# Two graph layers on one Trainium2 core: own issue tables for the second and the last-but-one graph, a last head in two pieces, an input check in steps, and sums scaled on GpSimd

## The chip, the core and the metric

The kernel runs on one core of one Trainium2 chip. The metric is the time of one execution in microseconds (us), as the device measures it; the time before is the median of three runs. Beside it there is one execution taken by the hardware profiler, and every duration below comes from that one.

The engines are named as in the profile: PE is the matrix engine (PEld its loading of weights), DVE the vector engine, ACT the scalar engine, POOL the GpSimd engine, and SP the engine from whose queue the DMAs of this kernel are issued. Each engine takes its instructions strictly in the order in which they were issued to it, and an instruction that waits holds up everything behind it on the same engine.

## The reference

There are 16 graphs of 1024 nodes with 256 features, and an adjacency matrix of integers for each. Two layers follow each other, each with a residual and a normalisation over the features.

```python
# layer 0: gated sum over all nodes; the gate depends on the kind of the edge
e = leaky(einsum('bid,bjd->bij', h * a[:, 0], h))          # four of these, a0 to a3
alpha = sigmoid(where(adj == 1, e0, where(adj == 2, e1, ... , neg_inf)))
x = layernorm(x + einsum('bij,bjd->bid', alpha, h) + bias)
# layer 1: graph attention with 4 heads of 64 features
Wh = (x @ W).reshape(B, N, 4, 64)
s = leaky_relu(e_src[:, :, None, :] + e_dst[:, None, :, :], 0.2)
alpha = softmax(where(A > 0, s, -1e9), axis=2)
x = layernorm(x + elu(einsum('bijh,bjhf->bihf', alpha, Wh)))
```

The adjacency of the data holds zeros and ones only and is symmetric. The kernel has a fast path for that, notes during the run whether the inputs allow it, and reads one flag at the end; if the flag is set, a general path computes everything again. With these data the flag is clear.

## The kernel before

**Stages and tables.** `stages` (L194) holds, for one graph, about fifty generators, one for each step of the work: `score`, `leak`, `leaky`, `sigmoid`, `below`, `lower`, `upper`, `self_loop` and `agg` for layer 0; `project`, `wh`, `product`, `high`, `low`, `pos`, `acc`, `acc_low`, `acc_sum`, `total`, `weigh`, `divide`, `elu` and `join` for layer 1; `moments`, `gathered`, `spread`, `shift` and `norm` for the normalisations. A table gives for each step of each generator a place on a common axis. Graph `b` is moved by `b` times `PERIOD` (112.0), all steps of all graphs are sorted, and `issue` (L1290) runs them in that order. So the tables, written out by hand as numbers, decide the order of the instructions on each engine, and nothing is reordered later. Several graphs are in work at once: while one is in layer 1, the next one is in layer 0. Before the change there are three tables: `FIRST` for graph 0, `LAST` for graph 15, and `TIMES` for graphs 1 to 14.

**The softmax as two sums.** In layer 1 the exponential of the leaky sum is one of two products, depending on whether the sum is positive. `pos` (L659, DVE) writes a 128 x 512 tile of zeros and ones for a head, half of the nodes and a block of 128 neighbours. `acc` (L671, PE) multiplies it with the factors `gm`, which hold a high and a low part of each number. `acc_low` (ACT) and `acc_sum` (L694, DVE) add the two parts into the tile `u`. The two PSUM tiles of `acc` are given back by these two steps, and the next head's first matmul needs them. `pos` has six buffers.

**The steps that the change touches in the middle graphs.** For each half of the nodes and each of its two pairs of blocks, `weigh` subtracts (L752 or L777) and then multiplies the second sum with `rho`; `divide` adds the sums (L787), takes the reciprocal of the denominator (L790, L792) and multiplies the sum with it; `elu` (L809, ACT) and `join` (L801, L803, DVE) follow. Both multiplications are the function `times`:

```python
if late:    # the last two graphs
    ... nc.scalar.activation(val[:, q, h, :], val[:, q, h, :], AF.Copy, scale=by[:, q, h : h + 1])
else:
    by = by.unsqueeze(3).to_broadcast(list(val.shape))
    nc.vector.tensor_tensor(val, val, by, ALU.mult)          # L769
```

So a graph has eight of these instructions on DVE, four on 128 x 520 numbers and four on 128 x 512, and graphs 0 to 13 have 112.

**GpSimd.** Apart from a few instructions that make constants, POOL runs only `spread` (L468 and L469), which turns four variances into four reciprocal square roots: twice in each layer of each graph.

**The last graph.** It computes layer 1 in another way: `pos_last` (L862) writes weights in full precision, `acc_last` (L872) multiplies them with the head's factors into a 65 x 512 sum, `kept_last` (L884, ACT) copies it, `turned_last` (L890, PE) turns it in four blocks, `inverse_last` (L904, L905), `scale_last` (L923, ACT), `elu_last` (L940), `join_last` (L947, L949) follow, and then the normalisation: four nodes' blocks at a time, with `spread` on POOL.

**The check.** After all graphs the kernel compares three kinds of numbers with their limits (L1470 to L1488: the sums of the adjacency and of its square, the span of the scores, the largest reciprocal), turns the result across the partitions on PE, and writes `flag`. Every engine then loads the flag (L1490) and branches over the general path.

Of the kernel before, what the change touches and what calls it, by code (L numbers as in the profile page):

```python
# [21 lines left out]
EPS = 1e-5  # L22
# [25 lines left out]
def make_constants(nc, k, const, work):  # L48
    D = k.D
    k.ident = const.tile([P, P], F32, name="ident")  # L50
    make_identity(nc, k.ident)
    k.ident16 = const.tile([P, P], BF16, name="ident16")
    make_identity(nc, k.ident16)
    k.mhalf = const.tile([P, 1], F32, name="mhalf")
    nc.gpsimd.memset(k.mhalf, -0.5)
    k.ones_r = const.tile([P, P], F32R, name="ones_r")
    ones = work.tile([P, P], F32, tag="ones", name="ones")
    nc.gpsimd.memset(ones, 1.0)
    nc.scalar.copy(k.ones_r, ones)
    k.ones = k.ones_r.bitcast(F32)  # L60
    k.w_aug = const.tile([P, k.DC, k.WD], F32, name="w_aug")
    k.bias_bc = const.tile([P, D], F32, name="bias_bc")
# [131 lines left out]
def stages(nc, k, pl, b, xg, adjg, outg, sums, span, zinv):  # L194
# [297 lines left out]

    def yt():
# [265 lines left out]
    def times(val, by):  # L759
# [7 lines left out]
        else:  # L767
            by = by.unsqueeze(3).to_broadcast(list(val.shape))
            nc.vector.tensor_tensor(val, val, by, ALU.mult)  # L769
# [87 lines left out]

    def pos_last():
        for half, h in LAST_HEADS:
            for jb in range(NB):  # L860
                p_ = t["pos", half, h, jb] = pl.pos.tile([P, HALF], F32, tag="pos", name="pos")
                nc.vector.scalar_tensor_tensor(  # L862
                    p_, t["sbc", half, h], t["es"][:, 1, jb, h : h + 1],
                    t["mT"][:, jb, half * HALF : (half + 1) * HALF], ALU.max, ALU.mult,
                )
                yield

    def acc_last():
        for half, h in LAST_HEADS:
            acc = t["acc", half, h] = pl.ps_u.tile([P, 2, HALF], F32, tag="u", name="acc")  # L870
            for jb in range(NB):
                nc.tensor.matmul(  # L872
                    acc[0 : F + 1, 0, :],
                    lhsT=factor_of(h)[:, jb],
                    rhs=t["pos", half, h, jb],
# [5 lines left out]
    def kept_last():  # L881
        for half, h in LAST_HEADS:
            kept = t["kept", half, h] = pl.allm.tile([P, HALF], F32, tag="allm", name="kept")
            nc.scalar.copy(kept[0 : F + 1, :], t["acc", half, h][0 : F + 1, 0, :])  # L884
            yield

    def turned_last():
        for half, h in LAST_HEADS:
            for q in range(NQ):
# [10 lines left out]
    def inverse_last():  # L900
        t["rz"] = pl.small.tile([P, H, NB], F32, tag="rzs", name="rzs")
        for half, h in LAST_HEADS:
            rz = t["rz"][:, h, half * NQ : (half + 1) * NQ]
            nc.vector.tensor_scalar(rz, sums_of(half, h)[:, :, F], Z_MIN, None, ALU.max)  # L904
# [47 lines left out]
    def leave():  # L952
        for half in range(NH):
# [5 lines left out]
            if half == NH - 1:  # L959
                z = zinv.rearrange("p b h -> p h b") if last else zinv  # L960
                nc.vector.tensor_tensor(z, z, t["rz"], ALU.max)
            yield

# [16 lines left out]
        spread1=spread("1"), shift1=shift("1"), norm1=norm("1"), leave=leave(),  # L980
# [110 lines left out]
FIRST = {  # L1091
    "aload": [-146.50, -146.40, -145.60, -145.40, -145.20, -144.50],
    "cast": [-146.00, -145.00, -144.10, -143.30, -142.40, -141.30, -140.80, -140.10],
    "turn": [-145.50, -144.80, -144.00, -143.00, -141.90, -140.90, -140.30, -139.30],
    "mask": [-145.10, -144.30, -142.70, -142.60, -141.20, -140.50, -139.70, -139.00],
    "setup": [-145.90, -142.90, -140.70],
    "xt": [-147.40, -147.20, -146.90, -146.80],
    "xtc": [-147.10, -146.70, -146.30, -146.10],
    "xta": [-146.60, -145.70, -144.70, -143.40, -141.50, -140.90, -139.60, -138.50],
    "score": [  # L1100
        -146.20, -144.90, -144.40, -143.70, -143.10, -142.30, -142.00, -141.80, -140.40,
        -139.10, -138.80, -137.70,
    ],
    "leak": [
        -145.80, -144.60, -143.90, -143.50, -142.80, -142.20, -141.40, -140.60, -140.00,
        -138.40, -138.10, -137.30,
    ],
    "leaky": [
        -145.30, -144.20, -143.60, -143.20, -142.50, -141.70, -141.00, -140.20, -139.40,
        -138.30, -137.60, -137.20,  # L1110
    ],
    "sigmoid": [-143.80, -142.10, -138.70, -137.80, -136.80, -136.70, -135.00, -134.80],
    "below": [
        -141.60, -140.00, -139.80, -139.30, -138.20, -137.10, -136.90, -136.60, -135.50,
        -134.60,
    ],
    "lower": [
        -141.10, -139.90, -139.50, -139.20, -137.00, -136.50, -136.40, -135.70, -134.90,
        -132.90,
    ],  # L1120
    "upper": [-138.90, -138.00, -136.30, -136.10, -135.20, -134.30, -134.20, -133.50],
    "self_loop": [-138.60, -137.50, -135.90, -135.40, -134.40, -133.30, -133.10, -131.70],
    "agg": [
        -137.90, -137.40, -136.20, -136.00, -135.80, -135.30, -134.50, -133.80, -133.60,
        -133.20, -133.00, -132.50, -132.20, -132.10, -131.90, -131.00,
    ],
    "residual": [-135.10, -134.70, -133.70, -132.70, -132.40, -131.60, -131.50, -130.60],
    "moments0": [-134.10, -133.90, -132.80, -132.60, -132.00, -131.20, -130.90, -130.40],
    "gathered0": [-134.00, -133.40, -132.30, -131.80, -131.10, -130.80, -130.50, -130.30],
    "spread0": [-131.40, -130.20],  # L1130
    "shift0": [-130.70, -130.10],
    "norm0": [7.49, 11.45, 12.49, 14.06, 21.08, 21.77, 22.17, 22.85],
    "yt": [14.24, 15.43, 27.38, 35.27],
    "ytc": [15.41, 16.39, 32.39, 35.36],
    "project": [17.27, 20.15, 20.63, 24.57, 36.07, 38.58, 38.81, 39.38],
    "wh": [19.92, 22.85, 25.81, 38.31, 39.70, 40.91, 43.46, 43.97],
    "sources": [38.35, 46.03],
    "rows": [43.24, 51.84],
    "keep_rows": [45.15, 52.35],
    "top_dve": [45.01, 46.50, 47.61, 48.41, 49.75],  # L1140
    "top_pe": [45.82, 47.95],
    "exps": [51.68],
    "product": [52.32, 52.36, 52.37, 53.07, 63.87, 68.87, 72.31, 73.12],
    "high": [52.66, 57.11, 58.54, 59.47, 64.43, 71.46, 73.63, 73.77],
    "low": [52.78, 60.94, 63.75, 65.98, 71.42, 75.46, 76.38, 76.38],
    "sload": [51.46, 76.59, 85.09, 91.68, 106.17, 107.86, 110.47, 136.87],
    "pos": [
        53.05, 53.94, 55.95, 56.21, 60.10, 62.46, 65.45, 71.47, 77.25, 79.42, 80.89,
        82.78, 83.73, 83.95, 84.83, 86.14, 90.35, 93.70, 95.10, 97.25, 100.20, 100.26,
        100.53, 101.07, 101.54, 102.14, 105.04, 105.05, 107.28, 107.74, 109.84, 110.83,  # L1150
        111.71, 112.48, 113.18, 113.44, 113.67, 113.82, 114.79, 114.95, 115.63, 116.01,
        116.29, 119.02, 119.40, 119.57, 123.16, 125.66, 125.90, 129.79, 135.31, 135.38,
        135.49, 144.04, 144.31, 144.39, 150.58, 150.96, 151.37, 151.47, 152.09, 153.82,
        156.33, 159.00,
    ],
    "acc": [
        64.31, 64.33, 64.82, 66.99, 68.04, 68.13, 72.21, 72.73, 82.68, 83.92, 84.06,
        84.17, 84.52, 85.29, 85.87, 90.42, 98.90, 99.90, 100.11, 100.56, 101.86, 101.99,
        103.90, 107.23, 109.46, 109.84, 109.87, 110.77, 110.96, 111.47, 111.56, 112.15,
        113.16, 113.39, 113.41, 113.83, 113.90, 116.39, 118.74, 119.06, 120.58, 120.70,  # L1160
        120.73, 122.19, 125.58, 125.72, 126.59, 126.65, 143.09, 143.39, 143.62, 146.56,
        146.86, 147.00, 147.26, 150.56, 154.28, 154.94, 159.15, 159.54, 163.16, 163.45,
        163.52, 164.31,
    ],
    "acc_low": [
        76.82, 78.61, 91.08, 96.03, 107.30, 107.72, 112.55, 112.62, 119.17, 119.31,
        129.75, 130.41, 152.88, 153.40, 166.46, 167.63,
    ],
    "acc_sum": [
        79.30, 79.99, 96.53, 96.98, 108.00, 108.36, 113.04, 113.14, 119.33, 119.48,  # L1170
        133.11, 134.38, 153.08, 153.64, 167.03, 171.24,
    ],
    "all_edges": [
        -17.80, 14.43, 80.16, 81.76, 83.98, 86.65, 96.10, 97.63, 105.44, 108.89, 112.81,
        114.68, 116.57, 122.61, 123.60, 125.76,
    ],
    "total": [
        76.70, 76.74, 79.15, 80.47, 81.48, 81.58, 82.30, 82.77, 84.60, 87.23, 93.78,
        95.95, 100.66, 101.42, 106.65, 108.21, 108.63, 109.34, 109.96, 113.70, 114.02,
        114.52, 115.05, 118.61, 121.02, 121.80, 122.87, 122.89, 126.17, 126.42, 126.44,  # L1180
        127.20,
    ],
    "total_kept": [81.08, 84.43, 98.17, 110.29],
    "total_less": [114.96, 118.68, 124.32, 127.71],
    "weigh": [120.62, 129.10, 191.46, 192.47, 198.84, 202.85],
    "divide": [
        123.90, 124.39, 125.72, 125.87, 130.47, 136.40, 142.86, 143.34, 204.10, 204.20,
        210.02, 212.01, 212.63, 216.15, 216.46, 217.58,
# [350 lines left out]
```

## Time and profile before

| | us |
|---|---|
| time, median of 3 runs | 1730.02 (1729.57 to 1730.39) |
| the profiled execution | 1729.9 |
| its span, first to last instruction | 1728.1 |
| PE busy | 1697.6 (98%) |
| DVE busy | 1623.3 (94%) |
| ACT busy | 1211.9 (70%) |
| POOL busy | 108.7 (6%) |
| L769, 112 instructions on DVE | 38.6 + 38.3 |

The time of an execution is the span and 1.8 us around it. A busy share is a mean over stages that are limited by different things: the first 100 us and the last 30 us have their own limits, and between them there is a long stretch in which each graph takes the same time as the one before it. A busy PE is one whose matmuls lie end to end; whether it is also waiting is read from the waits.

### The profile page before, as it was taken

To read this page: it belongs to the slowest core of one execution; us is meant where nothing else is said; L and a number is where in the kernel's file an instruction comes from. 1 tells how busy PE (TensorE), PEld (TensorE's weight loads), DVE (VectorE), ACT (ScalarE), POOL (GpSimd) and SP (SyncE) were. 2 spreads that over 40 slices of the span, in tenths; PEclk is the share of its full clock that TensorE was granted. 3 is DMA by queue.
4 is the path that set the end of the run, shared out by engine and by line. 5 is a ranking of instruction groups with operands and counts; after the bars stand their busy time and mean duration, and the time that the engine had idled before them with its cause. 6 is when DMAs were issued, how large, how long until landed. Compare 5 with 4: busy or idle time off the path is not lost.

```text
span 1728.1 us, 29041 instructions
## 1 busy us (share of the span) xinstructions
PE 1697.6 (98%) x10356; PEld 1459.7 (84%) x10356; DVE 1623.3 (94%) x3612; ACT 1211.9 (70%) x2679; POOL 108.7 (6%) x138
## 2 busy tenths in 40 slices
PE   8999999999999999999999999999999999999996
PEld 5789898998979989898998989989898898989932
DVE  5498999999999999999999999999999999999996
ACT  7674957859587685967859577695876859587553
POOL 0000000010000100001010000100001010000100
PEclk9999999999999999999999999999999999999998
DMA  5442433434324352343434424353343423432020
GB/s 194 126 116 68 99 98 92 111 92 121 101 78 107 99 141 71 100 118 90 113 92 98 113 78 110 98 126 88 96 101 102 125 68 86 122 86 56 20 74 26
DMA packets 249003, 168.56 MB, mean 98 GB/s; under 512 B 133010, under 2 KB 232468, under 8 KB 248852
## 3 DMA queue, kind: packets, MB, share of 16 engines
q1 hardware_dynamic: 248848, 166.63, 36.8%
q8 instruction: 84, 1.38, 0.3%
q14 instruction: 67, 0.55, 0.1%
q10 hardware_dynamic: 4, 0.00, 0.0%
HBM read 118.10 MB, written 17.04 MB: 78 GB/s over the span
## 4 chain that ended last, share of the span: by engine, by line
PE 89%; issue 6%; DVE 1%; DMA 1%; ACT 1%; POOL 1%; SPq 0%; POOLq 0%; DVEq 0%; ACTq 0%
PE acc L671 26%; PE agg L427 25%; PE tot L714 14%; PE e L356 13%; PE pw L517 6%; PE pg L395 3%; PE pt L498 1%; PE pt L319 1%; DMA sbc<-sdram 1%; POOL rstd L469 0%; DVE pos L659 0%; DMA aT<-a 0%; PE pbc L596 0%; ACT mT L298 0%; DVE gate L376 0%
## 5 line engine op out<-in xcount | busy, mean ns | idle before, releaser
L659 DVE SCALAR_TENSOR_TENSOR pos<-sbc,nd,mT 128x512 fp32r<-128x512 f32 x960 | 688.0, 738 | 9.1 <-DMA sbc<-sdram 4.9
L671 PE MATMUL acc<-gm,pos 128*128 128x260 f32 x3840 | 569.9, 291 | 0.0
L671 PEld LDWEIGHTS acc<-gm,pos 128*128 128x128 f32 x3840 | 500.6, 189 | 9.8 <-issue 1.0
L427 PE MATMUL agg<-xb,gate 128*128 128x256 f32 x2048 | 463.4, 379 | 0.1
L427 PEld LDWEIGHTS agg<-xb,gate 128*128 128x128 f32 x2048 | 379.8, 190 | 47.8 <-DVE gate L419 1.2
L714 PE MATMUL tot<-gm,allm 128*128 128x264 f32 x1920 | 309.3, 297 | 0.4 <-DVE gm L638 0.4
L714 PEld LDWEIGHTS tot<-gm,allm 128*128 128x128 f32 x1920 | 263.6, 189 | 4.2 <-DVE gm L638 0.6
L356 PE MATMUL e<-xT,xTa 128*128 128x512 f32 (+3 forms) x768 | 263.0, 487 | 2.5 <-ACT xTa L344 1.4
L356 PEld LDWEIGHTS e<-xT,xTa 128*128 128x128 f32 x768 | 134.7, 190 | 105.9 <-issue 55.0
L686 ACT COPY low<-acc 128x260 f32<-128x260 f32 x240 | 84.3, 377 | 177.0 <-PE acc L671 176.9
L489 ACT ACTIVATE y<-y,shift,rstd 128x256 f32<-128x256 f32 x254 | 136.4, 592 | 52.8 <-DVE shift L477 52.8
L706 ACT CAST allm<-mT 128x512 fp32r<-128x512 uint8 x240 | 147.6, 615 | 27.9 <-PE tot L714 26.6
L276 ACT ACTIVATE a<-a 128x1024 bf16<-128x1024 int32 x124 | 131.3, 1059 | 30.6 <-DMA aT<-a 21.6
L298 ACT ACTIVATE mT<-aT 128x1024 uint8<-128x1024 bf16 x120 | 127.2, 1060 | 6.5 <-DMA aT<-a 6.4
L468 POOL TENSOR_SCALAR std<-mv 128x4 f32<-128x4 f32 x64 | 28.4, 444 | 1605.1 <-DVE mv L450 1484.0
L517 PE MATMUL pw<-w_aug,yT 128*128 128x264 f32 x512 | 122.2, 387 | 0.5 <-ACT yT L507 0.5
L376 DVE TENSOR_TENSOR gate<-e,gate 128x512 f32<-128x512 f32 x192 | 104.1, 549 | 13.3 <-ACT gate L368 13.2
L444 DVE BATCH_NORM_STATS2 st<-y 128x6 f32<-128x256 f32 x256 | 105.7, 415 | 1.1
L517 PEld LDWEIGHTS pw<-w_aug,yT 128*128 128x128 f32 x512 | 93.0, 190 | 15.4 <-ACT yT L507 2.0
L694 DVE TENSOR_TENSOR u<-acc,low 128x260 f32<-128x260 f32 x240 | 95.6, 419 | 10.9 <-ACT low L686 10.8
L368 ACT ACTIVATE gate<-e 128x512 f32<-128x512 f32 x192 | 90.2, 486 | 15.8 <-PE e L356 15.4
L412 DVE TENSOR_TENSOR gate<-gate,mT 128x1024 f32<-128x1024 f32 (+7 forms) x128 | 95.6, 748 | 2.6 <-ACT mT L298 2.1
(122 smaller groups left out, 1880.5 us busy)
## 6 DMA issues: line engine op xcount, KB each, us to landing
a<-in_adj_dram SPq DMA_DIRECT2D x124, 512.0 KB, 4.8
sbc<-sdram SPq DMA_DIRECT2D x128, 256.0 KB, 4.7
out_dram<-y SPq DMA_DIRECT2D x31, 512.0 KB, 3.4
xb<-in_x_dram SPq DMA_DIRECT2D x15, 1024.0 KB, 5.5
a_us<-in_adj_dram SPq DMA_DIRECT2D x4, 512.0 KB, 8.6
aT<-a SPq DMA_TRANSPOSE x120, 3.1
xb<-in_x_dram SPq DMA_DIRECT2D x2, 512.0 KB, 4.5
sdram<-srow SPq DMA_DIRECT2D x32, 8.0 KB, 1.4
```

The lines of the kernel that those rows point to most:

```text
L276: nc.scalar.activation(t["a16", ib], t["a32", ib], AF.Copy, accum_out=sums[:, 0, at : at + 1])
L298: nc.scalar.activation(t["mT"][:, :, ib * P : (ib + 1) * P], t["aT", ib], AF.Square, accum_out=sums[:, 1, at : at + 1],)
L356: nc.tensor.matmul(e[:, 0:n], lhsT=t["xTa", jb][:, c, :], rhs=t["xT"][:, c, at : at + n], start=(c == 0), stop=(c == DC - 1),)
L376: nc.vector.tensor_tensor(ge, t["e", jb, at][:, 0:n], ge, ALU.max)
L427: nc.tensor.matmul(agg[:, 0:D], lhsT=t["gate"][:, jb, ib * P : (ib + 1) * P], rhs=t["xb"][:, jb, :], start=(jb == 0), stop=(jb == NB - 1),)
L444: nc.vector.bn_stats(st, t["y", half][:, q, :])
L489: nc.scalar.activation(y, y, AF.Identity, bias=shift, scale=rstd)
L517: nc.tensor.matmul(pw[:, 0:WD], lhsT=t["yT"][:, c, jb * P : (jb + 1) * P], rhs=k.w_aug[:, c, :], start=(c == 0), stop=(c == DC - 1),)
L659: nc.vector.scalar_tensor_tensor(p_, t["sbc", half, h], t["nd"][:, jb, h : h + 1], t["mT"][:, jb, half * HALF : (half + 1) * HALF], ALU.is ...
L671: nc.tensor.matmul(t["acc", half, h, q // 2][:, q % 2, 0 : 2 * E], lhsT=t["pos", half, h, jb][:, q * P : (q + 1) * P], rhs=pl.gm[:, h, jb] ...
L706: nc.scalar.copy(m_, t["mT"][:, j0 : j0 + 4, ib * P : (ib + 1) * P])
L714: nc.tensor.matmul(tot[:, 0 : H * F1], lhsT=t["allm", ib, jb // 4 * 4][:, jb % 4, :], rhs=pl.gm[:, :, jb, l, F:E], start=(jb == 0 and l == 0),
```

## The change

1. `times` multiplies on GpSimd instead of DVE in graphs 0 to 13, which the change counts as 1 to 14.
2. Graph 1 has a table `SECOND` and graph 14 a table `NEXT`; `FIRST` and `LAST` hold new numbers too. `TIMES` is unchanged, and now orders graphs 2 to 13.
3. In the last graph the last head of the second half is computed in two pieces of 256 nodes.
4. The last normalisation works on three groups of blocks (4, 2 and 2). The last group takes its square root on ACT and its reciprocal on DVE; a small square root ahead of it loads the ACT table. The output of these groups leaves in three DMAs.
5. The check becomes a generator, `verdict`, whose eight steps have places in `LAST`; its last part multiplies two columns of results on PE instead of a transpose and two reductions.

```diff
@@ times
-            nc.vector.tensor_tensor(val, val, by, ALU.mult)
+            nc.gpsimd.tensor_tensor(val, val, by, ALU.mult)
@@ issue
-        table = FIRST if b == 0 else LAST if b == len(graphs) - 1 else TIMES
+        own = {0: FIRST, 1: SECOND, len(graphs) - 2: NEXT, len(graphs) - 1: LAST}
+        table = own.get(b, TIMES)
@@ the last head in pieces
+    PIECES_LAST = [
+        (half, h, slice(c * HALF // n, (c + 1) * HALF // n))
+        for half, h in LAST_HEADS
+        for n in ((2 if (half, h) == LAST_HEADS[-1] else 1),)
+        for c in range(n)
+    ]
...
-        for half, h in LAST_HEADS:
+        for half, h, cols in PIECES_LAST:
...
@@ the last normalisation
+    GROUPS = [(0, NQ), (NQ, NQ + 2), (NQ + 2, NB)]
+    def warm_last():
+        junk = small("junk1", 1, bufs=1)
+        nc.scalar.activation(junk, k.eps, AF.Sqrt)
+        yield
+    def spread_last():
+        for a, b in GROUPS:
...
+            if b == NB:
+                nc.scalar.activation(rstd, var, AF.Sqrt, bias=k.eps)
+                nc.vector.reciprocal(rstd, rstd)
+            else:
+                v = small("std1", NQ)[:, 0 : b - a]
+                nc.gpsimd.tensor_scalar(v, var, EPS, None, ALU.add)
+                nc.gpsimd.tensor_tensor(rstd, v, k.mhalf.to_broadcast([P, b - a]), ALU.pow)
...
@@ the check
+    def verdict():
...
+        nc.vector.tensor_tensor(fine[:, 2:3], fine[:, 0:1], fine[:, 1:2], ALU.mult)
+        yield
+        nc.vector.tensor_reduce(
+            worst[:, 3:4], t["rz"].rearrange("p a b -> p (a b)"), AX.X, ALU.max
+        )
+        yield
+        nc.vector.tensor_scalar(
+            fine[:, 3:4], worst[:, 3:4], worst[:, 2:3], ZINV_MAX, ALU.max, ALU.is_le
+        )
+        yield
+        count = bank("count")
+        nc.tensor.matmul(
+            count[0:1, 0:1], lhsT=fine[:, 2:3], rhs=fine[:, 3:4], start=True, stop=True
+        )
+        yield
+        nc.vector.tensor_scalar(flag, count[0:1, 0:1], P - 0.5, None, ALU.is_lt)
+        yield
@@ LAST, the end of two rows
-    "leave": [5093.75, 5602.55],
+    "leave": [5215.64, 5985.98, 5985.98],
+    "verdict": [4243.21, 5463.00, 5488.21, 5489.01, 5491.07, 5560.41, 5601.71, 6000.81],
```

In the order that results, the following moves bear on the prediction. In graph 0 the first `rows` is issued on PE right behind the sixteen matmuls of `project` instead of behind four transposes of the next graph, and on SP the first load of `sbc` comes right behind the store of `srow` instead of behind a DMA transpose. On SP the seven small loads of `setup` come ahead of the third adjacency load instead of in two groups behind the fourth and the eighth. On DVE the last instructions are now: the reciprocal of the last piece, two `gathered`, five instructions of `verdict`, the two `join_last` of 128 x 128, two `moments`, two `gathered`, a `shift`, one instruction of `verdict`, the reciprocal, the `shift`, two `norm`, and the flag. On POOL the eight multiplications of a period stand five ahead of the `spread` of two normalisations and three behind it.

## The prediction

> **What bounds the kernel now.** I read the page's shares first, then busy time by stretch, then the waits.
>
> ```profile
> span 1728.1 us, 29041 instructions
> core 0: us, PE busy (x) PEld busy (x) DVE busy (x) ACT busy (x) POOL busy (x), PEclk, DMA share, GB/s
> 0.00:81.00 81.00, 70.72 (x359) 52.91 (x360) 37.74 (x107) 55.52 (x116) 3.80 (x14) 1.00 0.54 159
> 81.00:185.55 104.55, 103.32 (x654) 92.00 (x653) 93.22 (x196) 65.29 (x148) 3.82 (x4) 1.00 0.37 91
> 394.77:499.30 104.53, 104.53 (x658) 92.43 (x658) 102.09 (x227) 75.90 (x166) 7.02 (x8) 1.00 0.38 102
> 1690.00:1728.10 38.10, 22.95 (x66) 7.53 (x64) 24.94 (x63) 11.96 (x32) 3.28 (x4) 0.83 0.09 30
> ```
>
> The third row is one graph of the long middle. PE is busy for all of its 104.53 us, DVE for 102.09, POOL for 7. PE is the bound, with DVE 2.4 us behind it. DVE's waits in that stretch:
>
> ```profile
> DVE u L694 <- ACT low L686: 0.7, 1, 0.7
> DVE gate L376 <- ACT gate L368: 0.5, 1, 0.5
> DVE pos L659 <- DMA sbc<-sdram: 0.5, 1, 0.5
> DVE shift L477 <- POOL rstd L469: 0.3, 1, 0.3
> ```
>
> They sum to 2.0 us, and PE has none. So work taken from DVE in the middle gains nothing, and more than some 2.2 us a graph added to it makes DVE the bound. Time to gain lies in the first 105 us and in the last 16, where PE stands still.
>
> **The multiplications on GpSimd.** The removed rows, and what POOL does now:
>
> ```profile
> L769 DVE TENSOR_TENSOR u<-u,rho 128x520 f32<-128x520 f32 x56 | 38.6, 689 | 0.1
> L769 DVE TENSOR_TENSOR u<-u,rzs 128x512 f32<-128x512 f32 x56 | 38.3, 683 | 0.5
> masks.py:199 POOL TENSOR_SCALAR_AFFINE_SELECT ident<-ident 128x128 f32<-128x128 f32 x1 | 0.3, 292 | 0.0
> L468 POOL TENSOR_SCALAR std<-mv x64: 227/302/1237, 55.1 to 1718.3; 128x4 f32<-128x4 f32 x64
> 150.41 0.68 DVE L787 TENSOR_TENSOR u<-u 128x512 f32<-128x512 f32 x1
> 149.94 1.24 POOL L468 TENSOR_SCALAR std<-mv 128x4 f32<-128x4 f32 x1 [83.05 <-DVE mv L450]
> ```
>
> DVE loses 8 x 0.60 = 4.8 us a graph (0.68 each, of which 0.08 overlaps its neighbour). The same work on POOL isn't in the trace. Its length d is bounded below by POOL's fixed 0.23 (fastest L468) plus the slope from 4 to 128 numbers, (0.292 - 0.227) / 124 = 0.5 ns each: 0.49 us for 512. Above, four times 0.292, once per input: 2.34. I take 1.15, by the row that reads a whole array, scaled to 512 with its fixed part (1.17). POOL's 9 us a graph fit beside its 7.
>
> Two things can cost time. First, the result comes later. In the period from 729 to 790 the eight producers end 2 to 14 us before the consumer that reads them (L787 or `elu`), except for three with 1 to 5 us; d - 0.68 = 0.5 us is covered. A `spread` queued behind a multiplication delays its `shift` by up to 0.5 us, which comes out of DVE's margin.
>
> Second, what DVE and POOL share. In the last two lines the addition on four numbers took 1.24 us instead of 0.23 and ended 0.09 after L787 (151.09), a DVE instruction with two inputs in SBUF. So POOL waits for such an instruction; whether DVE also waits for POOL this trace can't show, as POOL never reads more than a few numbers here. Bounds: DVE loses nothing (-4.8 us a graph) or stops for the whole of each POOL instruction, apart from what it has in hand with at most one SBUF input. Following DVE's sequence at the eight places, at d = 1.15 it would lose 0, 1.0, 0.7, 0.9, 0.3, 0.3, 1.1, 0.9: 5.2 us, or 8 x (d - 0.5). I take this end, as a resource that one waits for is likely to be waited for by the other. DVE's net is then +0.4 us a graph, within its margin of 2.25, and the middle stays at PE's 104.5. If the cover is gone: a graph gets longer by 8 (d - 0.5) - 4.8 - 2.25 = 8d - 11.05, zero at d = 1.38; every 0.1 us above costs 0.8 us a graph and 11 us over 14 graphs.
>
> The Trainium skill speaks against this part. "GPSIMD Engine Reference", section 4.1, gives elementwise work to VectorE as about twice as fast, and its section 3.1 has 4497 ns for an fp32 tensor_tensor of 2048 numbers, from which I estimate 1.12 us for 512. "SBUF — State Buffer", section "Who interferes with whom", says that a DVE instruction with two SBUF inputs and a GpSimd instruction reading SBUF block each other completely, whoever came first. The 1.24 us row agrees for one direction, no row shows the other; by the page DVE's net is +0.4 us a graph, without it -4.8, and the time is PE's in both.
>
> **The end.** The last accumulation ends at 1712.4. From there:
>
> ```profile
> 1712.42 0.58 ACT L884 COPY kept<-acc 65x512 f32<-65x512 f32 x1 [2.14 <-PE acc L872]
> 1716.19 0.26 DVE L947 SCALAR_TENSOR_TENSOR u<-u,y 128x128 f32<-128x128 f32 x1
> 1718.29 0.23 POOL L468 TENSOR_SCALAR std<-mv 128x4 f32<-128x4 f32 x1 [24.11 <-DVE mv L450]
> 1718.60 1.04 POOL L469 TENSOR_TENSOR rstd<-std,mhalf 128x4 f32<-128x4 f32 x1
> 1719.67 0.16 DVE L477 SCALAR_TENSOR_TENSOR shift<-mv,rstd 128x4 f32<-128x4 f32 x1 [1.47 <-POOL rstd L469]
> 1721.38 0.37 PE L1485 MATMUL pm<-ident,bad 128*1 128x128 f32 x1 [7.87 <-DVE bad L1483]
> 1722.11 0.14 DVE L1488 TENSOR_SCALAR flag<-good 1x1 int32<-1x1 f32 x1
> ```
>
> Step by step: `kept` on 256 columns 0.38 instead of 0.58 (as copies of 264 numbers, 0.372 at L746): -0.2. Two transposes fewer: -0.1. From there to the last `join`, one pair of blocks is scaled instead of two, and DVE is also given two `gathered` and five check steps, small instructions of 0.15 to 0.2 us: the last L947 starts at about 1714.75 instead of 1716.19, which is -1.4, with the 0.3 above. The statistics of two blocks, 1.05 instead of about 1.5: -0.45. POOL's pair and its hand-overs, 1.47, become a square root on ACT (0.21, small ACT rows) and a reciprocal (0.18, L905) with two hand-overs of 0.06: 0.51, so -0.95. After the shift come `norm` on DVE (0.73, as now) and the flag. L961, two reductions, L1482, L1483 and L1487, 1720.52 to 1722.11, are placed earlier or left out: 1.6 us less, of which 0.2 comes back as another instruction ahead of the `shift`: -1.4. Sum -4.2: the flag ends at about 1718.05 instead of 1722.25. Loading the flag, the branch and the end, 5.85 us, stay. The new ACT table's load, 1.28 as for L382 in this trace, would end at about 1716.45, and the square root wants it at 1716.48: just covered; uncovered it costs its lateness, up to 1.3. The last DMA was issued at 1720.98 and landed 2.1 later, before 1728; the three now leave earlier and stay under the branch.
>
> **The start and graph 14.** Graph 0's `rows` comes 0.44 earlier (four transposes, 74.35), the load of `sbc` passes a DMA transpose of 1.24 us in SP's queue, and DVE waited 1.57 us for such a load at 100.6. Between 78 and 102 DVE sets the pace, so not all arrives: -1.5 out of the 6 us that PE loses from 65 to 105. On the other side, `setup`'s seven small loads, 0.44 us each, push the third adjacency load from 2.9 to 6.0; with 8.6 to land, 14.6, where its cast starts at 14.74: covered with nothing to spare. Bounds: +1.5 to -4. `NEXT` fills some of the 1.5 us lost between 1546 and 1643: -0.5; the hole of 2.9 us before the first `acc_last` stays, as it hangs on `project` (1643.5) and the new order has fewer `acc` to put there.
>
> **Sum.** The profiled execution took 1729.9: its span 1728.1 and 1.8 around it. 1729.9 - 4.2 - 1.5 - 0.5 = 1723.7; the median is 0.1 above the profiled execution: 1723.8. A measurement can tell 0.2%, some 3.5 us, from no change.
>
> **Rival 1: GpSimd holds DVE up (slower).** The mechanism is the one above, with d over 1.38. The gain of 6.2 at the ends is used up at d = 1.435, and at 1.47 the kernel is 0.2% slower. At d = 1.75, the middle between my 1.17 and 2.34, it's 14 x 2.95 = 41 more: 1765; at 2.34, 14 x 7.67 = 107 more: 1831. For it: the 1.24 us row, a second input read with a stride of zero, and that 2.25 us of margin is little. Against it: the only row with a whole array needs 1.17. Chance 0.32.
>
> **Rival 2: small stalls.** DVE keeps up on average, but comes late at some places: PE's first matmul of a head was released by `acc_sum` with 0.36 to 1.2 us to spare at four heads, and `pos` was at least 0.37 ahead of `acc`. A DVE instruction held for 1 us there costs 0.3 to 0.6 us a graph, 4 to 8 us in all: 1728 to 1732. Chance 0.14, mostly no measurable change.
>
> **Rival 3: the ends bring little.** The table load is late, the check's small steps delay the join, or the third adjacency load comes late, so that at most 3 us remain: 1727 to 1731. Chance 0.08.
>
> **How the numbers follow.** Forecast 0.46: its own range is 1719 to 1727, with 0.43 faster and 0.03 the same. Rival 2 gives 0.02, 0.10 and 0.02, rival 3 gives 0.01, 0.06 and 0.01, rival 1 all slower: 0.46 faster, 0.19 same, 0.35 slower. The range goes down to 1718.5 (the start's -4 instead of -1.5, and as much again at the end, where small instructions may hide better than I count), and up to 1752, d = 1.63; above that is about half of rival 1.
>
> **What would show it.** The row of L826 on POOL gives d. In a middle graph, DVE's busy time falls to about 97, the period stays 104.5, and PE has no waits for `pos` or `u`. If DVE's two-input rows get longer or gaps open before them, DVE is held up; if the period exceeds 104.5 while DVE's busy time and gaps fill it, rival 1 is right. The flag should end 5.7 us after the last accumulation instead of 9.8, with POOL absent from the chain there. I'd be wrong altogether if the middle moved with d under 1.4, or if it got shorter than PE's 104.5.

## The result and the profile after

The changed kernel takes 1735.74 us (median of 7 runs) against 1730.39 us before (7 runs): a ratio of 1.0031, 95% interval 1.0021 to 1.0041. That is 5.4 us or 0.3% slower, small but outside the noise. The prediction was 1723.8 us with 0.46 on faster. The profiled executions give the same difference, 1733.5 against 1728.1 us of span.

The page of the changed kernel: its span, and the rows of the moved multiplication and of `pos`, the commonest DVE instruction (here L826 and L716).

```profile
span 1733.5 us, 29137 instructions
PE 1702.9 (98%) x10373; PEld 1461.4 (84%) x10373; DVE 1622.9 (94%) x3510; ACT 1216.0 (70%) x2683; POOL 254.9 (15%) x251
L716 DVE SCALAR_TENSOR_TENSOR pos<-sbc,nd,mT 128x512 fp32r<-128x512 f32 x960 | 718.4, 773 | 8.7 <-PE acc L728 8.5
L826 POOL TENSOR_TENSOR u<-u,rho 128x520 f32<-128x520 f32 x56 | 67.1, 1198 | 606.4 <-DVE u L834 352.4
L826 POOL TENSOR_TENSOR u<-u,rzs 128x512 f32<-128x512 f32 x56 | 82.1, 1465 | 349.1 <-DVE rzs L849 349.1
```

DVE lost 112 instructions of 0.68 us, some 77 us, and its busy time is what it was (1623.3 before): the mean `pos` went from 738 to 773 ns and all of them together from 688.0 to 718.4 us, and other instructions grew as well. Busy time by stretch, a graph of the long middle first, then the last one from its first project matmul to the end:

```profile
core 0: us, PE busy (x) PEld busy (x) DVE busy (x) ACT busy (x) POOL busy (x), PEclk, DMA share, GB/s
903.86:1008.73 104.87, 104.86 (x660) 92.50 (x658) 102.12 (x220) 76.12 (x165) 16.92 (x16) 1.00 0.39 101
1640.50:1733.45 92.95, 75.91 (x275) 35.10 (x273) 79.00 (x193) 48.13 (x142) 7.90 (x10) 0.95 0.16 47
```

A middle graph takes 104.87 us instead of 104.45, with eight multiplications fewer on DVE and the same DVE time. DVE's waits in that graph sum to 2.4 us, among them two of `pos` for `acc` that weren't there before:

```profile
DVE u L751 <- ACT low L743: 1.0, 2, 0.7
DVE pos L716 <- PE acc L728: 0.6, 2, 0.4
DVE gate L378 <- ACT gate L370: 0.5, 1, 0.5
DVE shift L479 <- POOL rstd L471: 0.3, 1, 0.3
```

Where DVE's time went is seen in the timeline of one place (start, duration; the figure behind the bracket is idle time before it):

```profile
1204.37 0.69 DVE L716 SCALAR_TENSOR_TENSOR pos<-sbc,nd,mT 128x512 fp32r<-128x512 f32 x1
1204.52 1.48 POOL L826 TENSOR_TENSOR u<-u,rzs 128x512 f32<-128x512 f32 x1 [2.49 <-DVE rzs L849]
1204.98 1.07 DVE L1033 TENSOR_TENSOR zinv<-zinv,rzs 128x32 f32<-128x32 f32 x1
1205.97 0.74 DVE L716 SCALAR_TENSOR_TENSOR pos<-sbc,nd,mT 128x512 fp32r<-128x512 f32 x1
```

GpSimd starts in the middle of a `pos`, which ends at 1205.06, and needs 0.94 us more, until 1206.00 (1.04 to 1.07 us is its length where it starts beside no such instruction). The maximum of 32 numbers, 0.18 us in the kernel before, stands there for 1.07 us and ends 0.05 us after GpSimd. A held instruction shows no gap ahead of it: it's booked as a long one.

The whole difference by stretches, from the same events in three traces (us; "ends only" is the first experiment, the changed kernel with its multiplications on DVE):

| stretch | before | after | ends only |
|---|---|---|---|
| start to graph 1's first `project` matmul | 168.56 | 168.45 | 168.32 |
| to graph 14's first `project` matmul | 1359.42 | 1364.46 | 1360.29 |
| to the last graph's first `acc_last` | 122.99 | 125.22 | 124.47 |
| to the end of its last accumulation | 61.41 | 63.48 | 63.51 |
| to the flag written | 9.87 | 5.30 | 5.30 |
| to the end | 5.81 | 6.54 | 6.13 |

The tail of the changed kernel, behind its last accumulation:

```profile
1721.65 0.37 ACT L954 COPY kept<-acc 65x256 f32<-65x256 f32 x1 [2.12 <-PE acc L941]
1723.87 0.29 DVE L1020 SCALAR_TENSOR_TENSOR u<-u,y 128x128 f32<-128x128 f32 x1 [0.36 <-ACT u L1013]
1725.52 0.30 ACT L507 ACTIVATE rstd<-mv,eps 128x2 f32<-128x2 f32 x1 [0.17 <-DVE shift L521]
1725.85 0.17 DVE L508 RECIPROCAL rstd<-rstd 128x2 f32<-128x2 f32 x1 [0.19 <-ACT rstd L507]
1726.77 0.14 DVE L1073 TENSOR_SCALAR flag<-count 1x1 int32<-1x1 f32 x1
```

POOL is no longer on the way to the flag (its pair for the second group runs earlier, from 1723.12 to 1724.14), the square root and the reciprocal take 0.5 us, and the load of the ACT table (1723.85 to 1725.13) is over before the square root starts at 1725.52. The flag is written 5.30 us after the accumulation's end instead of 9.87. So the 4.2 us that the prediction saw there are there, and some more; but each stretch between graph 1 and that point got longer.

### The profile page after: what moved, and what is told of

Same layout as the page of the kernel before. It is cut to its first block, busy times and chain, and to the rows that moved or that the text cites. A ratio compares the mean times of both kernels' runs of the same rounds, so it can differ in the third digit from the quotient of the medians.

```text
span 1733.5 us, 29137 instructions
## 1 busy us (share of the span) xinstructions
PE 1702.9 (98%) x10373; PEld 1461.4 (84%) x10373; DVE 1622.9 (94%) x3510; ACT 1216.0 (70%) x2683; POOL 254.9 (15%) x251
## 3 DMA queue, kind: packets, MB, share of 16 engines
q8 instruction: 84, 1.38, 0.3%
## 4 chain that ended last, share of the span: by engine, by line
PE 87%; DVE 7%; ACT 3%; issue 1%; DMA 0%; POOL 0%; DVEq 0%; ACTq 0%
PE agg L429 25%; PE acc L728 24%; PE tot L771 12%; PE e L358 11%; PE pw L574 6%; PE pg L397 2%; DVE pos L716 2%; PE acc L941 2%; PE pt L555 2%; PE pt L321 1%; DVE pos L929 1%; DVE gate L414 1%; ACT mT L300 0%; DVE gate L378 0%; DVE st L446 0%
## 5 line engine op out<-in xcount | busy, mean ns | idle before, releaser
L716 DVE SCALAR_TENSOR_TENSOR pos<-sbc,nd,mT 128x512 fp32r<-128x512 f32 x960 | 718.4, 773 | 8.7 <-PE acc L728 8.5
L826 POOL TENSOR_TENSOR u<-u,rho 128x520 f32<-128x520 f32 x56 | 67.1, 1198 | 606.4 <-DVE u L834 352.4
L826 POOL TENSOR_TENSOR u<-u,rzs 128x512 f32<-128x512 f32 x56 | 82.1, 1465 | 349.1 <-DVE rzs L849 349.1
```

The source lines that it names most:

```text
L716: nc.vector.scalar_tensor_tensor(p_, t["sbc", half, h], t["nd"][:, jb, h : h + 1], t["mT"][:, jb, half * HALF : (half + 1) * HALF], ALU.is ...
L826: nc.gpsimd.tensor_tensor(val, val, by, ALU.mult)
```

## The experiments

Ratios are to the kernel before, run on the same chip, with 95% intervals.

### Ends only, and GpSimd only

The change in two halves.

```diff
# ends only: the changed kernel with
-            nc.gpsimd.tensor_tensor(val, val, by, ALU.mult)
+            nc.vector.tensor_tensor(val, val, by, ALU.mult)
# GpSimd only: the kernel before with the opposite edit
```

> The changed kernel with its 112 multiplications back on DVE: the new tables, the pieces, the groups and the stepwise check alone. Theory A (the middle pays at one place: PE waits 0.3 to 0.4 us a graph for the diagonal step L421 behind a pos that GpSimd held up; the ends bring next to nothing on their own): the period is 104.45 us again, the time is 1735.7 - 12 x 0.43 = 1730.5, within 1.5 us of the kernel before. Theory B (the ends do bring the 6 us of the prediction, and GpSimd's instructions of graphs 0, 12 and 13 spoil them): 1724 to 1726. Theory C (the new tables themselves are slower): above 1732.

Measured: 1730.66 us, ratio 0.9999 (0.9990 to 1.0008).

> The kernel before with nothing changed but the 112 multiplications, now on GpSimd. Theory A: the period is 104.87 us from graph 2 on, 13 x 0.43 = 5.6 us more, 1736 in all. Theory B: more than that at both ends of the run, 1739 to 1742. If the two parts of the change do not influence each other, this time less that of the kernel before, and that of the other experiment less that of the kernel before, add up to the measured 5.4 us.

Measured: 1736.02 us, ratio 1.0031 (1.0019 to 1.0043), period 104.90 us.

The ends are worth nothing that can be told from noise (-1.7 to +1.4 us), and GpSimd alone is as slow as the whole change. The 6.2 us expected of the ends aren't there even without GpSimd.

### One half of the nodes on GpSimd

```diff
-            nc.vector.tensor_tensor(val, val, by, ALU.mult)
+            (nc.gpsimd if half == 1 else nc.vector).tensor_tensor(val, val, by, ALU.mult)
```

> The kernel before with only the multiplications of the second half of the nodes on GpSimd (four a graph; in a period they run first, long before the step L421 for which PE waits). DVE is held up by 0, 0.76, 0.26 and 0.46 us there in the changed kernel, and saves 4 x 0.6. Theory A (what counts is what lies between DVE's last wait and the diagonal step): period 104.45, time as before within 1 us. Rival (DVE's whole sum, or matmuls that slow down beside GpSimd's reads, so every multiplication pays its share): half of the 5.6 us, 1733.

Measured: 1731.59 us, ratio 1.0007 (0.9998 to 1.0016), period 104.54 us.

> The kernel before with only the multiplications of the first half of the nodes on GpSimd (the four that come last in a period, just ahead of the diagonal step L421). DVE is held up by 0.87, 0.86, 0.88 and 0.78 us and saves 4 x 0.6, so it comes to L421 1.0 us later than before. Theory A: all of the loss is here, period 104.85 or so, 1735 to 1736. Rival (each multiplication pays its share): 1733.

Measured, with `half == 0`: 1735.18 us, ratio 1.0024 (1.0015 to 1.0034), period 104.83 us.

Four of the eight instructions make nearly all of the loss: 0.38 us of a period, against 0.09 for the other four. They run between 76 and 100 us of a period, counted from its first `project` matmul; there DVE is held up by 0.88, 0.87, 0.88 and 0.79 us and saves 4 x 0.6. The other four hold it up by 0, 0.77, 0.26 and 0.46. What PE waits for is seen at the end of such a period. The first line is of the kernel before, the others are of the changed one: DVE's two `pos` take 2.14 us instead of 1.41, and a load of weights waits for the diagonal step L421.

```profile
1207.91 1.41 DVE L659 SCALAR_TENSOR_TENSOR pos<-sbc,nd,mT 128x512 fp32r<-128x512 f32 x2
1211.76 2.14 DVE L716 SCALAR_TENSOR_TENSOR pos<-sbc,nd,mT 128x512 fp32r<-128x512 f32 x2
1211.91 1.44 POOL L826 TENSOR_TENSOR u<-u,rzs 128x512 f32<-128x512 f32 x1 [5.91 <-DVE rzs L849]
1214.81 0.28 DVE L421 TENSOR_TENSOR gate<-gate,ident 128x128 f32<-128x128 f32 x1
1215.14 0.30 PEld L429 LDWEIGHTS agg<-xb,gate 128*128 128x128 f32 x2 [0.41 <-DVE gate L421]
```

PE's busy time shows little of this (104.86 of 104.87 us): these matmuls start 0.22 us apart and each is booked for 0.38, so a hold of 0.3 us hardly opens a gap. It is seen in their starts.

### The diagonal step sooner

```diff
 TIMES["self_loop"]
-    [-22.52, ..., 18.13, 24.49]
+    [-22.52, ..., 18.13, 22.65]
```

> The kernel before with all 112 multiplications on GpSimd, and with one number of TIMES changed: the last diagonal step of each graph (self_loop, 24.49) comes at 22.65, right behind the step that writes its input, some 4 us sooner on DVE; the order on PE stays. Theory A (the whole of the middle's loss is PE's wait for this one instruction, DVE has room everywhere else): period 104.45 to 104.6, 1730 to 1732. Rival (DVE as a whole is too late with GpSimd's port holds; the wait only moves to the next pos or acc_sum): period 104.8 or more, 1735 to 1736.

Measured: 1738.23 us, ratio 1.0039 (1.0026 to 1.0053), period 105.0 us. My theory in this form falls. The wait for L421 (L419 in this kernel) is gone, and others stand in its place. PE's weight loads between 600 and 1300 us, in the GpSimd-only kernel and then in this one:

```profile
PEld agg L427 <- DVE gate L419: 2.7, 6, 0.4
PEld pw L517 <- ACT yT L507: 1.4, 8, 0.2
```

```profile
PEld pw L517 <- ACT yT L507: 2.9, 12, 0.3
```

With PE's matmuls of a graph laid over those of before, the GpSimd-only kernel loses 0.31 us at 101 us of the period and at most 0.08 before; this one loses nothing there, but 0.16 us at 103, and 0.12 and 0.18 at 4 and 7 us of the next. A loss at so few places also speaks against matmuls that get slower beside GpSimd's reads. And the move itself costs nothing where the multiplications are on DVE: steady graphs take 104.43 us in the last run of "The start and the end, each alone". So it isn't one instruction; what fits is that DVE is late over a whole stretch, and whatever PE needs of it first pays. DVE's waits say where its room is: in the kernel before they end at 2, 22, 75 and 85 us of the period (0.3, 0.5, 0.75 and 0.2 us). From 75 us on there is next to none until the next graph, and there the four instructions make DVE 1.0 us later.

### Two of the four

```diff
+    (nc.gpsimd if half == 0 and which == "divide" else nc.vector).tensor_tensor(...)
```

> The kernel before with only two of the eight multiplications on GpSimd: the two of divide in the first half of the nodes, the last ones of a period (DVE held up by 0.88 and 0.78 us, less 2 x 0.6 saved: 0.46 us later in the stretch between DVE's wait at 75 us of the period and the next graph). The four of that half together made DVE 1.0 us later and cost 0.36 us a graph, so about 0.6 us of lateness is free there. Theory (DVE's lateness within that stretch counts, past what is free): period 104.45 to 104.55, 1730.5 to 1732 beside 1731 before. Rival (every multiplication there pays its share of the 0.36): period 104.65, 13 x 0.19 = 2.5 us more, 1733.5.

Measured: 1733.00 us, ratio 1.0013 (1.0004 to 1.0022). The steady period is 104.56, 0.11 us more than before: at the edge of the theory's 104.45 to 104.55, and not the rival's 104.65. The time doesn't decide between them: it is 0.7 to 3.8 us more than before, and 13 x 0.11 = 1.4 and the rival's 2.5 both lie in that. In the trace, three graphs near the start also take 105.5 to 106.4 us.

> The same with the two of weigh in the first half of the nodes (held up by 0.87 and 0.86 us, 0.53 us later). Theory: period 104.45 to 104.55, time as before within 1.5 us. Rival: period 104.65, 2.5 us more.

Measured: 1731.68 us, ratio 1.0004 (0.9995 to 1.0013), period 104.53 us.

In the steady graphs two cost 0.11 or 0.08 us and four cost 0.38: more than in proportion, as lateness past a free amount does. The free amount has no sharp edge, as 0.46 and 0.53 us of lateness already cost something. Why graphs 1, 3 and 4 pay more isn't shown, and it is one trace; in the other kernels graph 1 takes 104.9 to 105.8 us without GpSimd's multiplications.

### GpSimd beside an unchanged DVE

The multiplications stay on DVE; GpSimd reads each result into a tile that nobody reads.

```diff
             nc.vector.tensor_tensor(val, val, by, ALU.mult)
+            out = junk.rearrange("p (q h f) -> p q h f", q=2, f=F)    # bf16
+            nc.gpsimd.tensor_tensor(out, val[..., 0:F], val[..., 0:F], ALU.mult)
+            # or, with one input: nc.gpsimd.tensor_copy(out, val[..., 0:F])
```

> The kernel before with its multiplications on DVE as they were, and behind each one a GpSimd instruction that multiplies the result with itself into a tile that nobody reads (512 numbers, bf16 out): GpSimd's holds without DVE's saving. Theory A (while GpSimd reads, a DVE instruction with two SBUF inputs stands still): DVE's busy time rises by about the 4.9 us a graph that the changed kernel shows, to 107, which is over PE's 104.5: period 107 to 109, 1765 to 1790. Rival (DVE's longer rows in the changed kernel are waits for GpSimd's results, not for a port): nothing reads these results, so the period stays 104.5 and the time is 1730 to 1732.

Measured: 1783.22 us, ratio 1.0297 (1.0281 to 1.0313), period 108.37 us.

> The same, but GpSimd copies the result into the unread tile: one input instead of two. Theory A (any read of SBUF by GpSimd holds DVE up): as with two inputs in proportion to the instruction's length, period 105 to 109. Rival (only a GpSimd instruction with two SBUF inputs holds DVE up): period 104.5, 1730 to 1732.

Measured: 1742.09 us, ratio 1.0063 (1.0048 to 1.0079), period 105.2 us.

Nobody waits for these results, and in such a graph DVE has 0.7 us of waits, none of them for GpSimd. So what slows DVE is GpSimd's work beside it. That it is the reading, and not the writing of the unread tile, isn't separated here. One place, and a graph by stretch, both of the kernel with two inputs:

```profile
1185.41 1.04 POOL L773 TENSOR_TENSOR junk<-u 128x512 bf16<-128x512 f32 x1 [25.55 <-DVE u L770]
1185.59 1.41 DVE L660 SCALAR_TENSOR_TENSOR pos<-sbc,nd,mT 128x512 fp32r<-128x512 f32 x1
```

```profile
1147.22:1255.59 108.37, 105.78 (x660) 92.42 (x659) 107.14 (x228) 76.00 (x165) 18.49 (x16) 1.00 0.38 98
```

DVE's busy time rose from 102.2 to 107.14, 4.9 us for eight instructions, and with it over PE's 104.45; now DVE is the bound, and PE stands still 2.6 us a graph. With one input GpSimd's instruction takes 0.61 us at its shortest instead of 1.03, DVE's busy time rises by 1.2 to 1.6 us, and PE loses 0.75.

### The start and the end, each alone

> The kernel before with the new start alone (the new FIRST, and SECOND for graph 1). Theory A: graph 1's project is 0.2 us earlier, graphs 3 and 4 take 105.2 us instead of 104.5, as DVE comes late to the diagonal step L421; 1731 to 1732. Rival (the prediction's -1.5): 1728.5.

The new `FIRST` and `SECOND` alone: 1731.51 us, ratio 1.0007 (0.9998 to 1.0016). PE stands still for 10.6 us of the first 110 instead of 11.5, and graph 1's `project` is 0.3 us earlier, which is less than such traces differ among themselves; but graphs 2 and 4 take 105.15 and 105.13 us instead of 104.50 and 104.47. The gain is given back.

> The kernel before (multiplications on DVE, FIRST and TIMES as they were at the start) with the new end alone: NEXT, the new LAST, the pieces, the groups, the stepwise check. In the trace of the ends-only kernel the last graph's first project matmul came 2.8 us late, the flag fell 4.5 us sooner after the last accumulation, and 1.7 us of lag had come from graphs 0 to 12. Theory A (the new start costs as it lets DVE lag in graphs 2 to 4, the new end gains what is left of it): 1728.0 to 1729.3. Rival (start and end are both worth nothing): 1730 to 1731.

The new `NEXT` and `LAST`, with the pieces and the stepwise check, alone: 1729.71 us, ratio 0.9997 (0.9988 to 1.0006). Within what can be told from no change; its trace is shorter by 0.8 us.

> The changed kernel with its multiplications on DVE and the last diagonal step of each graph of TIMES right behind its input (22.65). Theory A (the new start lost its gain in graphs 2 to 5 because DVE lagged at this step, and the new end is worth 1.7 us): the time of the ends-only kernel less 1.5 to 2 us, 1727.5 to 1729, below the kernel before by 0.1 to 0.2%. Rival (the lag of graphs 2 to 5 has another place): as the ends-only kernel, 1730 to 1731.

Ends only, with the last diagonal step in `TIMES` sooner: 1730.73 us, ratio 0.9997 (0.9988 to 1.0006), the same as without. The theory was wrong here too: graphs 2 and 4 still take 105.2 and 105.0 us, so the lag at the start doesn't hang on this step. Its place stays open.

### The last head whole, and graph 14 in the old order

```diff
-        for n in ((2 if (half, h) == LAST_HEADS[-1] else 1),)
+        for n in (1,)          # nothing at the places of the second piece
```

> As the kernel with the new end alone, but with the last head of the last graph whole: eight pos of 512 columns at the places of the first piece's, nothing at the second's. Theory A (the end is DVE's: sixteen pos of 256 take 7.0 us where eight of 512 take 5.4, and the pieces bring the last accumulation 2 us later for 0.3 to 1.4 us saved behind it): 1 to 2 us faster than with the pieces, 1726.5 to 1728. Rival (the pieces hide the first half's work beside the accumulation, as the prediction had it): 1 us slower than with the pieces.

Measured: 1730.29 us, ratio 0.9998 (0.9989 to 1.0007), against 0.9997 with the pieces. Theory A's gain isn't there; the rival's 1 us can't be told from these times. The traces can be laid side by side from the first `acc_last` on. There the accumulation takes 61.67 us with the head whole and 63.49 with the pieces, and from its end to the flag it is 8.60 and 5.30 us. So the pieces put 1.8 us ahead of the accumulation's end and take 3.3 from behind it: 1.5 us for them in this trace, as the rival has it. PE waits between the two pieces, here in the kernel with the new end alone:

```profile
1711.85 0.60 PE L941 MATMUL acc<-pos,fb 128*65 128x256 f32 x2
1713.57 2.37 PE L941 MATMUL acc<-pos,fb 128*65 128x256 f32 x10 [1.12 <-ACT u L996]
```

> As the kernel with the new end alone, but with graph 14 in the order of TIMES. Theory A (NEXT itself costs: graph 15's first project stood 2.8 us later with it, and its first pos 1.5 us later): 1 to 1.5 us faster, 1727 to 1728. Rival (NEXT fills holes, as the prediction had it): 0.5 us slower or more, as the new LAST was written to fit it.

Measured: 1765.65 us, ratio 1.0207 (1.0193 to 1.0221). PE stands still for 45 us instead of 22 with `NEXT`, all of the growth after 1540. The new `LAST` is written for the order of `NEXT`, so this tells how tightly two tables hang together, and not what `NEXT` costs.

### The tail by itself

The kernel before, its tables untouched.

```diff
 spread, last half of the last graph
-            nc.gpsimd.tensor_scalar(v, mvh[:, :, 1], EPS, None, ALU.add)
-            nc.gpsimd.tensor_tensor(rstd, v, k.mhalf..., ALU.pow)
+            nc.scalar.activation(rstd, mvh[:, :, 1], AF.Sqrt, bias=k.eps)
+            judge()            # zinv, worst, bad, the transpose
+            nc.vector.reciprocal(rstd, rstd)
 spread, first half of the last graph
+            judge_early()      # sums, span
 shift
+            judged()           # good, flag
```

> The kernel before, all tables and multiplications as they were, with two things changed behind the last accumulation: the last square root on ACT and its reciprocal on DVE instead of the pair on POOL, and the check ahead of the last norm (the sums and the span at the first normalisation of the last graph, the last reciprocals and the transpose while ACT takes the root, the flag behind the shift). Nothing ahead of the last accumulation moves. Theory (the new end loses ahead of the accumulation's end what it saves behind it, and the saving can be had by itself): flag 2 us sooner, 1.5 to 2 us faster than before, 0.1%. Rival (what follows the flag waits for DVE's last norm and the output anyway): no change.

Measured: 1733.76 us, ratio 1.0016 (1.0007 to 1.0025), slower. The flag came 2.4 us sooner after the last accumulation (7.44 against 9.87 us), as expected, and two things took it away:

```profile
1694.75 0.38 PE L471 MATMUL pmore<-more,ones_r 128*128 128x1 f32 x2 [2.36 <-DVE more L469]
1723.82 0.14 DVE L492 TENSOR_SCALAR flag<-good 1x1 int32<-1x1 f32 x1
1723.89 0.72 DVE L530 TENSOR_SCALAR y<-y,rstd,shift 128x256 f32<-128x256 f32 x2
```

The check's first matmul stands where PE has to wait 2.4 us for DVE, in the middle of the last accumulations. And from the flag to the end it now takes 7.19 us instead of 5.81, with DVE's `norm` behind the flag. Whether the saving can be had without a loss elsewhere stays open; this run shows that it isn't the flag alone that sets the end.

## Why the prediction was wrong, step by step

**The length d of a multiplication.** Right: 1.15 expected; 1.04 to 1.07 us where no DVE instruction holds GpSimd up, 1.44 and more where it first waits for one. The row that was named as the sign holds both: its means are 1.20 and 1.47 us.

**What DVE loses.** Right in sum: 5.2 us a graph expected at d = 1.15. In the changed kernel the lengthened instructions add up to 0 + 0.77 + 0.26 + 0.46 + 0.88 + 0.87 + 0.88 + 0.79 = 4.9 us. The bound taken, full blocking in both directions, is what the runs show. It is also what the Trainium skill's "SBUF — State Buffer", section "Who interferes with whom", states. The sign to look for was wrong, though: I said that busy time would fall to 97. It stayed at 102, as held time counts as busy.

**"Within its margin of 2.25, and the middle stays at PE's 104.5".** This is the step that failed in the middle. DVE's net was about 0, and the period still grew by 0.43 us, 5.0 us from graph 1 to 14. The margin was a sum over a whole graph, and it lay where DVE waits, at 2, 22 and 75 us; in the stretch behind those the four instructions cost 1.0 us net, of which 0.38 reached the period. By the same token the four that come early in a period gain nothing by what they save: DVE only waits longer there (`pos` for `acc`, 0.6 us a graph). The prediction also said that it would be wrong altogether if the middle moved with d under 1.4, and that is what happened.

Rival 2 had this mechanism and its size, 4 to 8 us, at a chance of 0.14, and looked for it at `acc_sum` and `pos`; it came first at the diagonal step. Its 1728 to 1732 us were missed because the ends were counted in. Rival 1's formula has its zero at d = 1.38. The real d is below that, and DVE is in fact not the bound; where the multiplications stay on DVE and GpSimd works beside them, in the run with two inputs, it is.

**The end, -4.2.** The tail itself is -4.6 (9.87 to 5.30), so these steps were well sized. What failed is that they were taken from a last accumulation that stays where it was. Its end came 2.1 us later after the first `acc_last`: 1.8 us of that are the pieces, with PE's gaps of 0.46 and 1.12 us around them, and a new gap of 0.67 us further ahead stands in the kernel with the whole head too. And in the ends-only kernel the first `acc_last` came 1.5 us later after graph 14's `project`. The 5.85 us behind the flag are 6.06 to 6.13 in the kernels with the new end and the multiplications on DVE, and 5.6 to 6.1 in those with the old end; only the 6.54 of the changed kernel stands out. For the ends-only kernel the table's differences add up: -0.24 + 0.87 + 1.48 + 2.10 - 4.57 + 0.32 = 0.0.

**The start, -1.5.** Between 65 and 105 us PE stands still for 3.5 us in the kernel before, not for the 6 that the prediction read, and for 2.1 in all four kernels with the new start: 1.4 us gained, as expected, and DVE's wait of 1.57 us is gone. But ahead of 65 us PE stands still for 8.5 to 9.2 us in these four, and for 7.9 to 8.1 in the others; that side had been left at nothing, with 1.5 as its bound. And graphs 2 to 4 together take 314.7 to 315.0 us with the new start and the multiplications on DVE, against 313.5: there was no term for them. What in the new order causes either isn't shown.

**Graph 14, -0.5.** From graph 12's `project` to the first `acc_last` takes 332.9 us with the new end alone and 332.4 before: +0.5. Why isn't shown.

Taken together: -6.2 expected of the ends, -0.2 measured (0.9999, interval -1.7 to +1.4 us); 0 expected of the middle, 5.4 measured (1.0031, interval +3.3 to +7.4 us). The sum, 5.2, agrees with the 5.4 of the whole change.

## What to carry to other kernels

An engine's margin belongs to a place: list where it waits, and check an added delay against the next wait of that kind behind it, not against the graph's sum. A saving behind a bound stretch counts only if the stretch's end stays where it is, so follow what the same edit puts ahead of it. Here, moving two-input elementwise steps from DVE to GpSimd freed DVE of 4.8 us a graph and held it up for 4.9, as its next instructions mostly read two tiles in SBUF.

## What the runs showed of the hardware

While GpSimd multiplies (1.04 us for 512 numbers), a DVE instruction with two inputs in SBUF stands still until GpSimd is done, and one with an input in PSUM doesn't. All 128 of L461, which adds from PSUM, take 0.38 to 0.42 us in the changed kernel, as in the kernel before. One place: beside the 1.45 us of L826 below, the addition from PSUM (L461) takes its usual 0.41, and the `pos` behind it 1.20 instead of 0.74.

```profile
1174.96 1.45 POOL L826 TENSOR_TENSOR u<-u,rzs 128x512 f32<-128x512 f32 x1 [6.53 <-DVE rzs L849]
1175.42 0.41 DVE L461 TENSOR_TENSOR y<-agg,bias_bc 128x256 f32<-128x256 f32 x1
1175.76 1.20 DVE L716 SCALAR_TENSOR_TENSOR pos<-sbc,nd,mT 128x512 fp32r<-128x512 f32 x1
```

A GpSimd copy with one input, 0.61 us at its shortest, holds DVE up as well (1.2 to 1.6 us a graph for eight). It takes more than a busy GpSimd: in the kernel before, its power of four numbers (L469, 1.04 us at its shortest) leaves a `pos` that starts beside it at its usual length. And neither engine's hold shows as a wait in the profile: it is found only as an instruction that is longer than others of its kind.
